# Three more groups of expert weights loaded inside attention layer 3, and the later groups spread over the experts' pairs

## The chip, the cores and the metric

The kernel runs on one core of one Trainium2 chip. The time is device microseconds (us) of one execution of the whole program. The time before is the median of six runs. One more execution was profiled; its trace has a record of each instruction on each engine.

## The reference

The model has four layers over 4 sequences of 256 tokens with 256 features (1024 tokens in all). Each layer is an attention (or a grouped transform) and a feed-forward part, each added to the running `x`. The change touches only what lies around the last two: attention layer 3 and the mixture of 64 experts after it, of which each token uses 8:

```python
x = x + _L3_xattn_ref(_layernorm(x), ctx, seg_ids, W_kvc, W_dq, W_uq, W_qr, W_uk, W_kr, W_uv, W_o)
x = x + _L3_ffn_ref(_layernorm(x), gate_w, gate_proj_w, up_proj_w, down_proj_w)
# in _L3_ffn_ref, with h = 256, I = 96, E = 64, K = 8:
router_logits = x @ gate_w
routing_weights, selected = jax.lax.top_k(router_logits, K)
routing_weights = softmax(routing_weights)
hidden_sorted = repeat(x, K)[order]            # rows of all choices, sorted by expert
gate = ragged_dot(hidden_sorted, gate_proj_w, group_sizes)
up   = ragged_dot(hidden_sorted, up_proj_w, group_sizes)
down = ragged_dot(silu(gate) * up, down_proj_w, group_sizes)
out  = sum(down[unsort].reshape(-1, K, h) * routing_weights[..., None], axis=1)
```

## The kernel before

**Two ways of ordering.** Everything up to the end of attention layer 3 is written as many small threads (`Flow`, L115). A planner in Python runs them at build time with estimated durations: it picks the next step by due time and by when its inputs are ready, and so fixes the order of the instructions on each engine. Shared buffers are handed out by roles; a thread that needs one waits in the plan until one is free. The experts (`experts`, L1973) are written out by hand, in a fixed order on each engine.

**Staging slots.** The role `stg` (L456) has nine buffers of 128 partitions by 2056 floats (`NSTAGE` = 9; 2056 is 8 rows of 257). Weights of the layers are loaded into them, and later the slots serve as queries of layer 3 (`q0`, `q1`) and as `hx`, the normalized rows that GpSimd scatters. The part `hx` may take slots 0 to 6 (`HX` = 7). After layer 3 the pool of slots is closed, and the experts' pool `moe` (L1750) lies over the same memory.

**From layer 3 to the experts.** Each of eight tiles of 128 tokens ends attention 3 in `tile3` (L1583): router, places of the choices (`slots`), then `scatter` (L1668), which issues eight indirect DMAs on GpSimd (L1674), one per choice, that put the token's row into the HBM array `hs`, sorted by expert. There are 64 of them. `fill_rows` (L427) loads the rows of one pair of experts from `hs`; it waits for the scatters of the choices that can lie there. SP, the engine that issues most loads, has the first three of these at the end of its list for the layers. Then follows a short stretch (L1781 to L1798): VectorE computes `late` and `over`, PE sums `over` (L1786), ScalarE writes `left_i`, all engines branch on it (the branch is for choices that found no place), and VectorE and ScalarE turn the logits `lgs` into routing weights.

**The experts.** The 64 experts' weights come in 16 groups of 4 (`GROUP`); a group is two DMAs, gate and up (768 KB) and down (384 KB), into a tile of 128 partitions by 2560 floats. Groups 0 and 1 (`FIRST` = 2) are loaded inside layer 3 into dead tensors (`cx`, `ctxT` and the weights of the layer 2 feed-forward; `first_experts`, L1316). The others go into a ring of `WEIGHTS` = 6 tiles `wt`. The loop goes over 32 pairs of experts; pair p uses group p // 2. On PE a turn of the loop is: gate and up of pair p (L1991), transposes of pair p + 1 (L1852), down of pair p - 1 (L1933), the other part of up of pair p (L1924), the rest of down of pair p - 1 (L1939). ScalarE computes silu (L1995) and copies `hbT` (L1856) and the results `yb` (L2006, L2010); VectorE multiplies `act` (L1928, L2002). GpSimd writes the results of a pair with three indirect DMAs (L1944) into the HBM array `yd`.

What follows a pair is in `beside` (L1955): it issues on SP the rows of pair p + 6 (`AHEAD`), perhaps a group of weights, perhaps a load of finished results from `yd` (`load_results`, L1862), and on VectorE some sums. The group's index is

```python
k = FIRST + 3 + p if p < WEIGHTS - 3 else p // 2 + WEIGHTS if p % 2 and p > 3 else 0
```

so that groups 5, 6 and 7 go after pairs 0, 1 and 2, and groups 8 to 15 after pairs 5, 7, 9 and so on to 19. Groups 2, 3 and 4 are issued ahead of the loop by `experts`. SP takes its list in order: a row load that must wait for its buffer (the rows of pair p + 6 take the buffer of pair p, which the result DMAs of pair p read) holds back the groups behind it.

Of the kernel before, what the change touches and what calls it, by code (L numbers as in the profile page):

```python
# [28 lines left out]
P = 128  # L29
B, S, D = 4, 256, 256  # L30
NTOK = B * S
NT = NTOK // P
# [14 lines left out]
E3, I3, K3 = 64, 96, 8  # L47
# [12 lines left out]
NROWS = E3 * CAP  # L60
NPAIR = NTOK * K3
NSTAGE = 9
HX = 7
HW = D + 1


# [48 lines left out]
class Flow:  # L115
# [11 lines left out]
    def role(self, name, n, make=None):  # L127
        self.roles[name], self.makers[name] = [0.0] * n, make

    def part(self, name, role, n):  # L130
        self.parts[name] = role, n

    def slots(self, name):
        role, n = self.parts.get(name, (name, None))
        return self.roles[role][:n]

    def go(self, gen, due=0.0):
        th = Thread(gen, due)
        self.threads.append(th)
        self.resume(th, None)  # L140
        return th
# [15 lines left out]
    def start(self, op):  # L157
        t = self.free.get(op.engine, 0.0)
        for b in op.reads:
            if b.ready is None:  # L160
                return None
            t = max(t, b.ready)
        for b in op.writes:
            t = max(t, b.used, b.ready or 0.0)
        need = {}
        for spec in op.new:
            need[spec[0]] = need.get(spec[0], 0) + 1
        for name, n in need.items():
            times = sorted(x for x in self.slots(name) if x is not None)
            if len(times) < n:  # L170
                return None
            t = max(t, times[n - 1])
        return t

    def take(self, spec):
        name, args = spec[0], spec[1:]
        k = min((x, k) for k, x in enumerate(self.slots(name)) if x is not None)[1]
        name = self.parts.get(name, (name,))[0]
        self.roles[name][k] = None
        make = self.makers[name]  # L180
        return Buf(make(k, *args) if make else None, name, k)
# [50 lines left out]
def model(ctx: ExitStack, tc: tile.TileContext, a: dict, out: bass.AP):  # L232
    nc = tc.nc
# [14 lines left out]
    def held(pool, shape, name, dtype=F32):  # L248
        return pool.tile(shape, dtype, tag=name, name=name)
# [40 lines left out]
    q2 = [held(early, [P, 2 * I2], f"q2{k}", BF16) for k in range(3)]  # L290
    means = held(early, [P, 8], "means")
    wmask = held(early, [P, NT, S], "wmask", BF16)
    kvc = held(const, [P, NT, KVC3], "kvc")
    kpos = held(early, [P, S], "kpos")
    mid = held(early, [P, NT], "mid")
# [97 lines left out]
    def expert_sources(k):  # L393
        es = slice(k * GROUP, (k + 1) * GROUP)
        return a["w3_gu"][:, es, :, :], a["w3_dn"][:, es, :]
# [5 lines left out]
        )  # L401
    ]

    readers = []
    puts = [[] for _ in range(K3)]

# [28 lines left out]
    def layers(nk):  # L435
# [11 lines left out]
            )  # L447

        def stage_tile(k, name):
            return stage.tile([P, K3 * HW], F32, tag=f"stg{k}", name=name)  # L450

        flow.role("bank", 8, maker(banks, "bank"))
# [2 lines left out]
        flow.role("sc", 32, maker(acts, "sc"))  # L455
        flow.role("stg", NSTAGE, stage_tile)  # L456
        flow.part("hx", "stg", HX)
        flow.role("lane", LANES[0])
        flow.role("lane3", LANES[1])

# [33 lines left out]
        def loader():  # L494
# [10 lines left out]
                    queue.dma_start(dst, source)  # L505

            def stage_in(name, kb, pairs):
                b = yield Op(SP, 0.06, new=[("stg", name)], kb=kb)
                for dst, source in pairs(b.ap):
                    nc.sync.dma_start(dst, source)  # L510
                fill(name, b)
# [60 lines left out]
            )  # L572
            yield from put(WROT, nc.sync, 384, (wrot3, a["w3_qrot"]))
            yield from put(GATE3, nc.sync, 64, (gate3, parts_of("w3_gate", 2)))
            b = yield Op(None, 0.0, new=[("stg", "keys3")])
            fill("keys3", b)
            yield from stage_in(
                "wq3", 384,
# [9 lines left out]
                    for k, n in enumerate(("w3_ukT", "w3_uvT"))  # L588
                ],
            )  # L590
            b = yield Op(None, 0.0, new=[("stg", "bo3")])
            fill("bo3", b)
            for k in range(2):
                yield from stage_in(
# [721 lines left out]
        def first_experts():  # L1316
            yield Join([keys_thread])
            for parts, k in first_weights:
                yield Op(SP, 0.12, (), (CX, *CT, *Q2), kb=1152)
                for dst, source in zip(parts, expert_sources(k)):  # L1320
                    nc.sync.dma_start(dst, source)

        waiting = [2] * B

        before = [len(js) for js in puts]
        PUT = [Buf() for _ in range(K3)]

        def first_rows():
            for p in range(in_early - 1):
                yield Op(SP, 0.06, PUT[2 * p : 2 * p + 2], kb=386)  # L1330
                fill_rows(p, before)
# [356 lines left out]
        def attention3(b):  # L1688
            lane = yield Op(None, 0.0, new=[("lane3",)])
            q = yield Op(None, 0.0, new=[("stg", "q0"), ("stg", "q1")])  # L1690
            yield from queries3(b, q)
            left = [2]
            for k in range(2):
                go(tile3(2 * b + k, q, lane, left), due(b, "h3") + 15.0 * k)

        with tc.manual_schedule(engines=ORDERED | {mybir.EngineType.SP}):
            go(loader())
            if nk == 1:
                few_thread = go(few_rows(), due(0, "x0"))
            for c in range(NCH):  # L1700
                go(chunk(c), due(2 * c, "x0"))
            w = DUE_WEIGHTS
            go(fp8_weights(), w["fp8"])
            go(scaled_context(), w["f1"] - 20.0)
            go(ffn1_weights(), w["f1"])
            go(products2(), w["p2"])
            go(ffn2_weights(), w["f2"])
            go(windows(), w["win"])
            go(centred_gate(), w["win"])
            keys_thread = go(keys_values(), w["kv"])  # L1710
            go(products3(), w["p3"])
            go(first_rows())
            flow.run()

# [37 lines left out]
    def moe_tile(shape, tag, bufs):  # L1752
        return moe.tile(shape, F32, tag=tag, name=tag, bufs=bufs)

    diag = moe_tile([P, NT // 2, len(ON_PE), P], "diag", 1)
    wts = [moe_tile([P, GROUP * (4 * I3 + D)], "wt", WEIGHTS)]
    weights = [parts for parts, _ in first_weights]

    def load_weights(k):
        wt = wts.pop() if wts else moe_tile([P, GROUP * (4 * I3 + D)], "wt", WEIGHTS)  # L1760
        parts = expert_parts(wt[:, : GROUP * 4 * I3], wt[:I3, GROUP * 4 * I3 :])
        for dst, source in zip(parts, expert_sources(k)):
            nc.sync.dma_start(dst, source)
        weights.append(parts)


    def load_rows(p):
# [66 lines left out]
    silu = small.tile([P, 1], F32, tag="silu", name="silu", bufs=1)  # L1834
    eqs = moe_tile([P, K3, E3], "eqs", 1)
    backs, gats = [], {}
    n_pairs = E3 // 2

    def choice_weights(t):
# [22 lines left out]
    def load_results(js, p):  # L1862

        half = NT // 2
        for h in range(2):
            if js[0] in (0, 2, 3) and (h == 0 or js[0] == 0):
                g = moe_tile([P, GROUP * (4 * I3 + D)], "wt", WEIGHTS)[:, : NT * D]
            elif js[0] == 4:
                g = gats[0][h].rearrange("p t j d -> p (t j d)")
            elif js[0] == 6:  # L1870
                g = (cx.rearrange("p t d -> p (t d)"), ctxT.rearrange("p c r -> p (c r)"))[h]
            else:
                continue
            g = g.rearrange("p (t j d) -> p t j d", j=len(js), d=D)
            n = 2 if js[0] == 6 else g.shape[1]
            for j in js:
                gats.setdefault(j, []).append(g)
            for t0 in range(0, g.shape[1], n):
                at = (h * half + t0) * P * K3
                source = yd[at : at + n * P * K3, :].rearrange("(t p j) d -> p t j d", p=P, j=K3)  # L1880
                ld = nc.sync.dma_start(  # L1881
                    g[:, t0 : t0 + n].rearrange("p t j d -> p t (j d)"),
                    source[:, :, js[0] : js[-1] + 1, :].rearrange("p t j d -> p t (j d)"),
                )
                needs(ld, "back", backs[: RPP * (p + 1)], "results of these choices alone")
# [69 lines left out]
    def beside(p):  # L1955
        if p < 2 * NT and p % 2 == 0:
            choice_weights(p // 2)
        n, m = len(on_pe), n_pairs - 2 * NT
        for t, j in on_pe[max(p - 2 * NT, 0) * n // m : max(p - 2 * NT + 1, 0) * n // m]:
            nc.vector.tensor_scalar(  # L1960
                diag[:, t // 2, j - ON_PE[0], :], ident, choice_w[:, t, j : j + 1], None, ALU.mult
            )
        if p + AHEAD < n_pairs:
            load_rows(p + AHEAD)
        k = FIRST + 3 + p if p < WEIGHTS - 3 else p // 2 + WEIGHTS if p % 2 and p > 3 else 0
        if k and k < E3 // GROUP:
            load_weights(k)
        if p in loaded:
            load_results(loaded[p], p)
        for t, j in added_at.get(p, ()):  # L1970
            add_result(t, j)

    def experts():  # L1973
        load_weights(FIRST)
        for p in range(in_early - 1, AHEAD):
            load_rows(p)
        load_weights(FIRST + 1)
        load_weights(FIRST + 2)

        nc.scalar.activation(silu, mhalf, AF.Silu)  # L1980
        nc.vector.tensor_mul(lgs, lgs, wide(kept))
# [148 lines left out]
```

## Time and profile before

| | us |
|---|---|
| median of 6 runs | 687.32 (685.62 to 689.4) |
| profiled execution, whole | 686.86 |
| its span from first to last instruction | 685.1 |
| PE matmul busy | 595.5 (87%) |
| VectorE, ScalarE, GpSimd busy | 427.1, 376.8, 411.5 |
| attention layer 3 ends, last scores (L1526) | 460.9 |
| last scatter ends on GpSimd (L1674) | 493.6 |
| first pair's gate and up (L1991) | 490.5 |
| last pair's gate and up (L1991) | 646.3 |

The share of the span that an engine is busy is a mean over stages with different limits; the windows view gives it by stretch. A row of the waits view says which engine's instruction on which line waited, and for what. A wait for several things is put down to the one that came last. Matmul ends are modelled. The granted clock of PE is between 0.5 and 1.

### The profile page before, as it was taken

What the parts mean: (1) busy time and instruction counts of PE and PEld (TensorE: products, weight loads), DVE (VectorE), ACT (ScalarE), POOL (GpSimd) and SP (SyncE); (2) the same over time, 40 slices, a digit from 0 to 9 for tenths busy, and PEclk for the clock granted to TensorE, in tenths of its full rate; (3) what the DMA queues carried; (4) which work ended last, traced back from release to release, by engine and by line L of the source; (5) the groups of instructions that cost most, each with busy time, mean ns of one, the idle gap of its engine ahead of it and who ended that gap; (6) DMA issues with size and microseconds to landing.
All of it is one profiled execution on the core that took longest, in us unless ns stands there. A gap on an engine that the chain in (4) does not pass through costs nothing. (4 is left out here: it accounts for less than half of the span.)

```text
span 685.1 us, 11045 instructions
## 1 busy us (share of the span) xinstructions
PE 595.5 (87%) x3703; PEld 451.8 (66%) x3716; DVE 427.1 (62%) x1063; ACT 376.8 (55%) x931; POOL 411.5 (60%) x531
## 2 busy tenths in 40 slices
PE   5997699989999999999999899496497998888936
PEld 4763376766887778778687678274375776766724
DVE  5789857875968795799785556353343453323625
ACT  1143258769788763667876875384344453434500
POOL 6997985044464536558268587727645666555860
PEclk9999999999999999999999999799599999999966
DMA  8999999501100230000031110202689788877376
GB/s 282 369 386 215 204 211 244 153 25 47 62 2 1 62 108 2 0 1 1 4 114 39 62 63 32 93 16 81 195 273 326 249 241 280 265 213 244 92 237 238
DMA packets 65250, 98.14 MB, mean 143 GB/s; under 512 B 7174, under 2 KB 51927, under 8 KB 65184
## 3 DMA queue, kind: packets, MB, share of 16 engines
q1 hardware_dynamic: 55264, 78.40, 40.0%
q0 software_dynamic: 7680, 16.84, 7.0%
q10 hardware_dynamic: 2240, 2.10, 0.9%
q8 instruction: 32, 0.52, 0.3%
q14 instruction: 34, 0.28, 0.1%
HBM read 58.42 MB, written 43.07 MB: 148 GB/s over the span
## 5 line engine op out<-in xcount | busy, mean ns | idle before, releaser
L1944 POOL DMA_INDIRECT yd<-yb,hb x84 | 92.2, 1098 | 52.1 <-issue 22.2
L1674 POOL DMA_INDIRECT hs<-hx,slots x64 | 66.0, 1032 | 26.0 <-issue 13.7
L881 POOL TENSOR_TENSOR st<-st,mhalf 128x1 f32<-128x1 f32 x56 | 33.0, 593 | 57.4 <-DVE st L877 43.5
L1928 DVE TENSOR_TENSOR act<-ps_u,g 64x192 f32<-64x192 f32 x64 | 22.7, 355 | 50.8 <-PE ps_u L1924 22.6
L1991 PE MATMUL ps_gu<-hbT,wt 128*128 128x192 f32 x224 | 44.4, 342 | 8.2 <-ACT hbT L1856 8.2
L1505 POOL TENSOR_TENSOR q<-rt 64x512 f32<-64x512 f32 x32 | 42.5, 1327 | 11.0 <-DVE rt L1501 7.7
L1991 PEld LDWEIGHTS ps_gu<-hbT,wt 128*128 128x128 f32 x224 | 35.9, 191 | 19.4 <-ACT hbT L1856 11.0
L1538 ACT ACTIVATE e<-ps_s,nm 128x128 f32<-128x128 f32 x128 | 45.6, 392 | 5.6 <-DVE nm L1532 4.8
L2002 DVE TENSOR_TENSOR act<-ps_gu,g 32x384 f32<-32x384 f32 x32 | 18.0, 562 | 41.0 <-ACT g L1995 31.5
L1995 ACT ACTIVATE g<-ps_gu 96x384 f32<-96x384 f32 x32 | 15.6, 487 | 42.6 <-PE ps_gu L1991 13.4
L1933 PE MATMUL ps_y<-wt,act 96*128 96x256 f32 x112 | 31.4, 406 | 8.4 <-DVE act L1928 6.6
L1526 PEld LDWEIGHTS ps_s<-keys,q 128*128 128x128 f32 x256 | 34.7, 197 | 1.4
L1526 PE MATMUL ps_s<-keys,q 128*128 128x128 f32 x256 | 34.6, 279 | 0.0
L1450 POOL TENSOR_TENSOR hh<-g,v 128x512 f32<-128x512 f32 x16 | 20.2, 1276 | 23.8 <-ACT g L1448 20.0
L1576 PE MATMUL ps_u<-e,kvc 128*64 128x512 f32 x64 | 22.8, 632 | 12.4 <-issue 10.1
L1856 ACT COPY hbT<-tp_hb 128x768 f32<-128x768 f32 x31 | 24.7, 798 | 14.7 <-PE tp_hb L1852 9.7
L1259 ACT ACTIVATE qT<-tp_q,rnd 128x512 bf16<-128x512 f32 (+2 forms) x48 | 25.7, 568 | 12.4 <-PE tp_q L1255 12.4
L1532 DVE TENSOR_REDUCE nm<-ps_s 128x4 f32<-128x512 f32 x32 | 21.5, 683 | 14.9 <-remote 11.2
L1491 PE MATMUL ps_q<-qc,wq 96*128 96x256 f32 x128 | 30.4, 380 | 0.0
L884 DVE TENSOR_SCALAR h<-x,st 128x256 f32<-128x256 f32 x56 | 27.0, 494 | 5.1 <-POOL st L881 4.8
L1163 ACT ACTIVATE e<-ps_s,nb 128x256 f32<-128x256 f32 x64 | 30.1, 494 | 0.0
L1562 ACT COPY e<-tp_e 128x512 f32<-128x512 f32 x32 | 18.5, 605 | 20.2 <-issue 10.4
(348 smaller groups left out, 1720.2 us busy)
## 6 DMA issues: line engine op xcount, KB each, us to landing
hs<-order SPq DMA_DIRECT2D x1, 12336.0 KB
hb<-hs SPq DMA_DIRECT2D x28, 385.5 KB
wt<-in_w_gu SPq DMA_DIRECT2D x14, 768.0 KB
yd<-order SPq DMA_DIRECT2D x1, 8192.0 KB
wt<-yd SPq DMA_DIRECT2D x6, 1024.0 KB
wt<-in_w_dn SPq DMA_DIRECT2D x14, 384.0 KB
wo<-in_w_o SPq DMA_DIRECT2D x2, 1024.0 KB
w<-in_w SPq DMA_DIRECT2D x2, 704.0 KB
```

Of the source, the lines that this page charges most:

```text
L881: nc.gpsimd.tensor_tensor(s[:, 8:9], s[:, 7:8], mhalf, ALU.pow)
L884: nc.vector.tensor_scalar(h[:, k, :], x_t(t), ss[k][:, 6:7], ss[k][:, 8:9], ALU.subtract, ALU.mult)
L1163: nc.scalar.activation(e[:, mt, :], s[:, mt, :], AF.Exp, bias=nb[:, mt : mt + 1], accum_out=tot[:, 2 * j + mt : 2 * j + mt + 1],)
L1259: nc.scalar.activation(qT[:, 4 * i : 4 * i + full, :], tp.ap[:, :full, :], AF.Identity, bias=rnd[:, 1:2])
L1491: nc.tensor.matmul(ps.ap[:, k, :], w[:, hp * P : (hp + 1) * P], qc.ap, start=True, stop=True)
L1505: nc.gpsimd.tensor_add(qv(q[i])[r, hps, :], t0[r], t1[r])
L1526: nc.tensor.matmul(s.ap[:, k, :], qv(q[hd % 2])[:, hd // 2, rows], keys3[:, hd % 2, b * S : b * S + nk * P], start=False, stop=k == n - 1,)
L1538: nc.scalar.activation(wide[:, k, :], s.ap[:, k, :], AF.Exp, bias=nm[:, k : k + 1], accum_out=tot[:, k : k + 1],)
L1674: put = nc.gpsimd.indirect_dma_start(out=hs[:, :], out_offset=bass.IndirectOffsetOnAxis(ap=slots[:, t, j : j + 1], axis=0), in_=rows[:, j, ...
L1933: nc.tensor.matmul(y[:, i], act[:, i, whole[i]], dn[:, i], start=True, stop=True)
L1944: put = nc.gpsimd.indirect_dma_start(out=yd[:, :], out_offset=bass.IndirectOffsetOnAxis(ap=hbs[p][:, j, D : D + 1].bitcast(I32), axis=0), ...
L1991: nc.tensor.matmul(ps[:, i], gu[:, i, dc, :P], hbT[:, dc, mine[i]], start=dc == 0, stop=dc == 1)
```

## The change

Four of the nine staging slots (7, 2, 6, 8, in this order) become one tensor, `deep`, that outlives the layers, so that three tiles of 2560 floats fit into it side by side. `more_experts` loads groups 2, 3 and 4 there inside layer 3: the first when slot 7 is given back, the second for slot 6, the third for slot 8, none before the queries of the last sequence are asked for (`ASKED`). So that the slots are free in time, `hx` may take only slots 0, 4 and 5, the kept tensors `keys3` and `bo3` slots 1, 3 and 5, and `wq3` slot 2. The ring of six tiles becomes a fixed list, `homes`: three in `deep` and three from the pool `moe`; group k uses home (k - 2) % 6. No group is issued ahead of the loop any more. Groups 5 to 15 are issued in `beside` after pairs 0, 3, 5, 8, 11, 14, 16, 19, 22, 24 and 27 (`round(2.7 * k)`). The tiles into which results are loaded come from the same list.

```diff
-HX = 7
+HX = (0, 4, 5)
+KEPT = (1, 3, 5)
+DEEP = (7, 2, 6, 8)
...
+    deep = held(early, [P, len(DEEP) * K3 * HW], "deep")
...
+    n_wt = GROUP * (4 * I3 + D)
+    homes = [deep[:, o : o + n_wt] for o in range(0, len(DEEP) * K3 * HW - n_wt + 1, n_wt)]
+
+    def home_parts(wt):
+        return expert_parts(wt[:, : GROUP * 4 * I3], wt[:I3, GROUP * 4 * I3 :])
+
+    def fetch(k, parts):
+        for dst, source in zip(parts, expert_sources(k)):
+            nc.sync.dma_start(dst, source)
...
         def stage_tile(k, name):
+            if k in DEEP:
+                o = DEEP.index(k) * K3 * HW
+                return deep[:, o : o + K3 * HW]
             return stage.tile([P, K3 * HW], F32, tag=f"stg{k}", name=name)
...
         flow.part("hx", "stg", HX)
+        flow.part("kept", "stg", KEPT)
+        flow.part("wq3", "stg", (2,))
+        for k in DEEP:
+            flow.part(f"deep{k}", "stg", (k,))
...
+        def more_experts():
+            for k, home in enumerate(homes):
+                taken = [f"deep{n}" for n in (DEEP[:1], DEEP[2:3], DEEP[3:])[k]]
+                yield Op(SP, 0.12, (ASKED,), new=[(n, "wt") for n in taken], kb=1152)
+                fetch(FIRST + k, home_parts(home))
...
             yield from queries3(b, q)
+            if b == B - 1:
+                ASKED.ready = flow.now
...
             go(products3(), w["p3"])
+            go(more_experts())
             go(first_rows())
...
-    wts = [moe_tile([P, GROUP * (4 * I3 + D)], "wt", WEIGHTS)]
+    homes += [moe_tile([P, n_wt], f"wt{k}", 1) for k in range(len(homes), WEIGHTS)]
     weights = [parts for parts, _ in first_weights]
-
-    def load_weights(k):
-        wt = wts.pop() if wts else moe_tile([P, GROUP * (4 * I3 + D)], "wt", WEIGHTS)
-        parts = expert_parts(wt[:, : GROUP * 4 * I3], wt[:I3, GROUP * 4 * I3 :])
-        for dst, source in zip(parts, expert_sources(k)):
-            nc.sync.dma_start(dst, source)
-        weights.append(parts)
+    weights += [home_parts(homes[k % WEIGHTS]) for k in range(E3 // GROUP - FIRST)]
...
+    free_homes = [homes[k % WEIGHTS] for k in range(E3 // GROUP - FIRST, E3 // GROUP - FIRST + 4)]
...
-                g = moe_tile([P, GROUP * (4 * I3 + D)], "wt", WEIGHTS)[:, : NT * D]
+                g = free_homes.pop(0)[:, : NT * D]
...
-        k = FIRST + 3 + p if p < WEIGHTS - 3 else p // 2 + WEIGHTS if p % 2 and p > 3 else 0
-        if k and k < E3 // GROUP:
-            load_weights(k)
+        if p in fetched:
+            fetch(fetched[p], weights[fetched[p]])
...
+    early_groups = FIRST + len(DEEP) - 1
+    fetched = {round(2.7 * k): early_groups + k for k in range(E3 // GROUP - early_groups)}
+
     def experts():
-        load_weights(FIRST)
         for p in range(in_early - 1, AHEAD):
             load_rows(p)
-        load_weights(FIRST + 1)
-        load_weights(FIRST + 2)
```

More of the change, by code (lines that the diff above doesn't have):

```diff
@@ L128, in role, with part @@
         self.roles[name], self.makers[name] = [0.0] * n, make
-    def part(self, name, role, n):
-        self.parts[name] = role, n
+    def part(self, name, role, ks):
+        self.parts[name] = role, ks
     def slots(self, name):
-        role, n = self.parts.get(name, (name, None))
-        return self.roles[role][:n]
+        role, ks = self.parts.get(name, (name, None))
+        times = self.roles[role]
+        return [(times[k], k) for k in (range(len(times)) if ks is None else ks) if times[k] is not None]
     def go(self, gen, due=0.0):
@@ L168, in start @@
         for name, n in need.items():
-            times = sorted(x for x in self.slots(name) if x is not None)
+            times = sorted(x for x, _ in self.slots(name))
             if len(times) < n:
@@ L176, in take @@
         name, args = spec[0], spec[1:]
-        k = min((x, k) for k, x in enumerate(self.slots(name)) if x is not None)[1]
+        k = min(self.slots(name))[1]
         name = self.parts.get(name, (name,))[0]
@@ L507, in stage_in @@
             def stage_in(name, kb, pairs):
-                b = yield Op(SP, 0.06, new=[("stg", name)], kb=kb)
+                b = yield Op(SP, 0.06, new=[("wq3" if name == "wq3" else "stg", name)], kb=kb)
                 for dst, source in pairs(b.ap):
@@ L574, in loader @@
             yield from put(GATE3, nc.sync, 64, (gate3, parts_of("w3_gate", 2)))
-            b = yield Op(None, 0.0, new=[("stg", "keys3")])
+            b = yield Op(None, 0.0, new=[("kept", "keys3")])
             fill("keys3", b)
@@ L590, in loader @@
             )
-            b = yield Op(None, 0.0, new=[("stg", "bo3")])
+            b = yield Op(None, 0.0, new=[("kept", "bo3")])
             fill("bo3", b)
@@ L1319, in first_experts @@
                 yield Op(SP, 0.12, (), (CX, *CT, *Q2), kb=1152)
-                for dst, source in zip(parts, expert_sources(k)):
-                    nc.sync.dma_start(dst, source)
+                fetch(k, parts)
+        def more_experts():
[3 more added lines that the diff above has]
+                fetch(FIRST + k, home_parts(home))
         waiting = [2] * B
+        ASKED = Buf()
         before = [len(js) for js in puts]
@@ L1755, in model @@
     diag = moe_tile([P, NT // 2, len(ON_PE), P], "diag", 1)
-    wts = [moe_tile([P, GROUP * (4 * I3 + D)], "wt", WEIGHTS)]
+    homes += [moe_tile([P, n_wt], f"wt{k}", 1) for k in range(len(homes), WEIGHTS)]
     weights = [parts for parts, _ in first_weights]
-    def load_weights(k):
-        wt = wts.pop() if wts else moe_tile([P, GROUP * (4 * I3 + D)], "wt", WEIGHTS)
-        parts = expert_parts(wt[:, : GROUP * 4 * I3], wt[:I3, GROUP * 4 * I3 :])
-        for dst, source in zip(parts, expert_sources(k)):
-            nc.sync.dma_start(dst, source)
-        weights.append(parts)
+    weights += [home_parts(homes[k % WEIGHTS]) for k in range(E3 // GROUP - FIRST)]
     def load_rows(p):
```

## The prediction

> **What bounds the kernel now.** I read the windows first (columns: stretch, its length, busy time with instruction count of PE, weight load, VectorE, ScalarE, GpSimd, then granted clock, DMA share, GB/s).
>
> ```profile
> 480.00:500.00 20.00, 10.65 (x48) 8.44 (x48) 6.82 (x15) 6.56 (x11) 11.31 (x21) 0.60 0.65 195
> 500.00:520.00 20.00, 17.66 (x123) 13.52 (x124) 9.04 (x18) 8.92 (x17) 11.38 (x12) 1.00 0.95 300
> 520.00:540.00 20.00, 16.14 (x113) 12.31 (x114) 8.48 (x17) 7.61 (x15) 10.90 (x12) 1.00 0.94 299
> 600.00:620.00 20.00, 16.39 (x113) 13.01 (x113) 5.49 (x16) 7.25 (x15) 10.75 (x12) 0.97 0.66 199
> ```
>
> To about 470 the layers run with PE 94 to 99% busy per 100 us from 100 to 400. The experts (488 to 660) are bound by PE too, but PE waits there, and at their start the DMA engines are full (0.95, 0.94). What PE waits for, from the waits view of 486 to 646 (us in total, times, longest):
>
> ```profile
> PE ps_gu L1991 <- ACT hbT L1856: 9.1, 7, 2.1
> PE tp_hb L1852 <- DMA q<-hs: 6.4, 1, 6.4
> PE tp_hb L1852 <- DMA hb<-hs: 2.7, 3, 1.7
> ...
> PE tp_hb L1852 <- DMA wmask<-hs: 0.9, 1, 0.9
> ```
>
> Then the timeline from layer 3 into the experts (start, duration, engine, line):
>
> ```profile
> 480.84 0.22 DVE L1781 TENSOR_TENSOR late<-tops,bound 128x64 f32<-128x64 f32 x1 [3.26 <-POOL tick L1673]
> 481.10 0.22 DVE L1784 TENSOR_REDUCE over<-late 128x8 f32<-128x64 f32 x1
> 483.37 0.69 DVE L1791 TENSOR_TENSOR q<-q,tops 128x512 f32<-128x512 f32 x1 [2.05 <-ACT left_i L1788]
> 488.21 0.69 DVE L1981 TENSOR_TENSOR q<-q,kept 128x512 f32<-128x512 f32 x1
> 490.51 0.56 DVE L1859 COPY hbT<-tp_hb 128x384 f32<-128x384 f32 x1 [1.61 <-issue]
> 490.53 2.93 PE L1991 MATMUL ps_gu<-hbT,cx 128*128 128x192 f32 x8 [0.57 <-issue]
> 492.60 0.98 POOL L1674 DMA_INDIRECT hs<-hx,slots  x1 [0.22 <-issue]
> 500.30 0.37 SPq L429 DMA_DIRECT2D wmask<-hs  x1
> ```
>
> The reader is to see: VectorE goes through `late` to L1981 (8.1 us) while GpSimd still issues scatters (the last ends at 493.58). Nothing in that chain waits for scatters to land. SP's load of pair 3 (`wmask`) does, and is issued only at 500.30.
>
> I call S(p) the start of pair p's first L1991. From S(9) = 538.35, S(10) = 542.60, S(11) = 546.86 an undisturbed pair takes 4.25 us. The sum is made against the profiled execution, 686.86 us (span 685.1 and 1.76 around it); the median of the runs, 687.32, lies 0.46 above.
>
> **What does not move.** In the built programs the instructions of PE, VectorE, ScalarE and GpSimd stand in the same order, and the planner gives the same staging slots to the same tensors. Cost to 480: nothing. What differs is SP's list and what some instructions wait for.
>
> **Three groups inside layer 3.** They sit in SP's list behind groups 0 and 1 and ahead of the first rows (issued 484.46). Their slots are last read by L1491 (412) and by the last scores, L1526 (460.9). A group takes about 6.5 us (issued at 593.70, hardware queue busy to about 600), DMA is 17% busy in 450 to 480, so all have landed by about 475. Cost nothing, hidden by SP's idle time before 484; were that cover gone, each group would put the first rows back by its 6.5.
>
> **Relief at the start.** Before, six groups leave SP from 492 to 518, mixed with the row loads; rows of pair 7, issued at 507.86, let PE start only at 524.46. After, no group is issued between layer 3 and `wmask`, rows of pairs 4 to 6 go next, and groups 5 and 6 follow. From S(0) = 490.53 to S(10) took 52.07. Without these waits it is 10.82 for the first two pairs (clock at 0.50 to 495) plus 8 x 4.25 = 44.8. So at most -7.2; the five waits that name rows or precede row-bound transposes (0.88, 0.61, 1.73, 1.09, 1.04) make -5.35. I take -6.3.
>
> **An added wait.** The experts' pool keeps three weight tiles instead of six, so its tiles sit elsewhere. In the built program the first VectorE instruction after layer 3, `late` (L1805 after), now waits for all eight counters of the scatters, six at their full count of 128, the last scatter's among them; before it waited for none. Queued behind it on VectorE are L1791 to L1798, L1981 and then L1859, the second half of `hbT` of pair 0. Waiting for those: the overflow matmul, which stands ahead of the first transposes on PE, ScalarE's exponentials, and the first L1991. So the experts cannot start before the last scatter has landed plus that chain.
>
> When does it land? GpSimd is done at 493.58. Upper bound: 500.2, where SP's 5.8 us wait for it ended before, with group 2's 1152 KB and 771 KB of rows on the same engines. Lower bound: rows of pairs 1 and 2 were issued 3.1 and 1.8 us after GpSimd ended the last scatter they need, so 495.4. Group 2 is gone, so I take 496.3, 2.7 after. The chain: 8.1 us at most (480.84 to 488.90), 6.1 if the 2.05 ahead of L1791, which no counter explains, passes during the wait. S(0) is then 502.4 to 504.4; I take 503.4, +12.9 on 490.53. Ends: 495.4 + 6.1 is +11.0, 500.2 + 8.1 is +17.8.
>
> **Later groups.** They are issued at p = 0, 3, 5, 8, 11, 14, 16, 19, 22, 24, 27, each behind the row load of p + 6, which waits until the results of pair p are written. Group 15 was issued after pair 19, used at 30. Those row loads left 13.5, 13.3, 11.4, 12.3, 14.4 and 10.6 after S(p+1) (p = 20 to 25), median 12.8; 0.5 for the issue and 5 for the gate and up part makes 18.3. Group 12 (p = 19, pair 24) has 4 x 4.25 = 17.0: 1.3 late. Group 13 (p = 22, pair 26) has 12.75: 5.5 late, but S(23) to S(26) took 16.60 anyway, leaving 1.65. Group 14 is covered by 13's delay; group 15 follows row load 31 (p = 25) and is in time. So 2.9 to 6.8; take +4. Bounds: 0 if results land in 10, and 10 with the clock's drop on two waits (after the 2.1 us wait at 576.37 the clock stood at 0.50 in 578 to 581, and S(17) to S(18) took 5.88, 1.6 too long).
>
> [...]
>
> **What stays.** S(10) to S(31) took 103.66 against 21 x 4.25 = 89.25: 14.4 of waits, mostly `hbT` from ScalarE, whose cause the rows do not show. From S(31) to the end, 38.8: result writes of GpSimd back to back from 634 to 664.7, then the loads of results. I keep both, within 4 either way.
>
> Sum: 686.86 + 12.9 - 6.3 + 4 = 697.5; on the median 697.9.
>
> **Rivals.** (1) Relief decides and it is faster. Place: scatters landing at 495.4, chain 6.1: +11.0; relief in full, -7.2; no late group; and half of the 14.4 gone, since three groups fewer share the engines: -7.2. That gives 683.5. It decides once waits of the stage fall by more than the 11.0 that the start loses. For it: DMA share 0.8 to 0.95 there. Against: S(9) to S(11) ran at 4.25 each with the DMA share at 0.79 (540 to 560). (2) The late groups become the bound: landing at 498 and chain 8.1 (+15.6), relief -5.35, late groups +10: 707. It decides if results land 14 us after S(p+1), as once. Against: the spread of the six. (3) The added wait is already met when VectorE gets there, so that only relief and late groups count: 686.86 - 6.3 + 4 = 684.6. Against: 480.84 lies 12.7 us ahead of the last scatter's issue.
>
> **How the numbers follow.** Forecast 0.76, rival 1 0.08, rival 2 0.13, rival 3 0.03. The forecast's own range is 690.7 to 704.1 (686.86 with 11.0 - 7.2 + 0 and with 15.6 - 5.35 + 7). To hold 8 in 10 it takes a part of rivals 1 and 2 at each end: 688.5 to 706. A difference of 0.3%, 2.1 us, is about what a measurement of this kernel can tell from none. Faster by more: rival 1 and 0.01 of rival 3, 0.09; within: 0.02 of rival 3 and 0.04 at the edge of the forecast, 0.06; slower 0.85.
>
> **What would show it.** Right: `late` starts at 495 to 498, S(0) at 502 to 505, no wait of L1852 for `hb` before pair 10, S(10) at 547 to 551, and PE waiting for weights (`ps_gu` behind `deep` or `wt` loads) around pairs 24 to 28. Wrong: `late` near 481, or S(0) within 5 us of 490.5; or a layer before 480 whose lines move; or S(10) to S(31) in under 96, which would be rival 1's saving.

## The result and the profile after

The changed kernel takes 705.64 us (median of 20 runs, 700.44 to 710.17) against 687.09 before; the ratio is 1.0289, 95% interval 1.0264 to 1.0314. On the 687.32 from which the forecast started that is 707.2, 1.2 above the upper end of the forecast range and 9.3 above the forecast of 697.9. The direction was right and the size was not. Times are us throughout. The profiled execution took 703.76, span 702.0.

The same four stretches as before, and one more behind them (stretch, length, PE, weight load, VectorE, ScalarE, GpSimd, granted clock, DMA share, GB/s):

```profile
480.00:500.00 20.00, 0.00 (x0) 0.01 (x1) 1.13 (x6) 2.47 (x3) 13.07 (x26) 0.50 0.48 150
500.00:520.00 20.00, 16.37 (x91) 12.30 (x92) 9.61 (x20) 9.53 (x16) 3.30 (x4) 0.76 0.90 269
520.00:540.00 20.00, 18.25 (x126) 14.42 (x127) 9.21 (x20) 8.64 (x17) 12.05 (x13) 1.00 0.15 50
600.00:620.00 20.00, 15.72 (x102) 12.59 (x99) 5.23 (x15) 6.75 (x13) 11.67 (x12) 0.91 0.70 231
...
636.00:643.00 7.00, 6.20 (x22) 5.28 (x24) 0.56 (x1) 1.56 (x3) 2.21 (x3) 0.51 0.75 243
```

PE does nothing at all from 480 to 500, where it was busy for 10.65 before. From 520 to 540 the DMA engines are nearly idle (0.15, before 0.94) and PE is busier (18.25, before 16.14). The last line is new: PE at half clock (0.51) late in the experts. The waits of 480 to 665 (us in total, times, longest) name both ends:

```profile
PE ps_over L1810 <- DVE over L1808: 20.5, 1, 20.5
...
DVE late L1805 <- DMA hs<-hx,slots: 18.8, 1, 18.8
...
PE ps_gu L2015 <- ACT hbT L1881: 10.1, 6, 4.3
...
PE ps_gu L2015 <- DMA wt<-in_w_gu: 4.0, 1, 4.0
...
PE ps_gu L2015 <- DMA deep<-in_w_gu: 3.6, 1, 3.6
```

The timeline from the last scatter to the first pair (L2015 is the gate and up line of after, L2005 the old L1981):

```profile
495.23 0.97 POOL L1701 DMA_INDIRECT hs<-hx,slots  x1 [0.23 <-issue]
498.87 0.36 SPq L443 DMA_DIRECT2D wmask<-hs  x1
499.39 0.23 DVE L1805 TENSOR_TENSOR late<-tops,bound 128x64 f32<-128x64 f32 x1 [18.77 <-DMA hs<-hx,slots]
...
504.21 1.01 PE L2015 MATMUL ps_gu<-hbT,cx 128*128 128x192 f32 x2 [0.57 <-ACT hbT L1883]
...
504.61 0.69 DVE L2005 TENSOR_TENSOR q<-q,kept 128x512 f32<-128x512 f32 x1
```

The last scatter ends on GpSimd at 496.20; 3.2 later `late` runs, and 4.8 after that PE starts pair 0. With S(p) read from the rows of L1991 and L2015, the difference of the two profiled spans (16.9) splits like this; the last column repeats it for a second trace of each kernel, both taken on one chip in the same group of runs:

| stretch | before | after | difference | forecast | second pair of traces |
|---|---|---|---|---|---|
| to S(0) | 490.53 | 504.21 | +13.7 | +12.9 | +10.8 |
| S(0) to S(10) | 52.07 | 48.02 | -4.1 | -6.3 | -3.7 |
| S(10) to S(31) | 103.66 | 114.05 | +10.4 | +4 | +10.0 |
| S(31) to the end | 38.84 | 35.72 | -3.1 | 0 | -1.2 |

### The profile page after: what moved, and what is told of

Its sections match the earlier page's. It is cut to its first block, busy times and chain, and to the rows that moved or that the text cites. A ratio compares the mean times of both kernels' runs of the same rounds, so it can differ in the third digit from the quotient of the medians.

```text
span 702.0 us, 11054 instructions
## 1 busy us (share of the span) xinstructions
PE 600.1 (85%) x3703; PEld 455.3 (65%) x3716; DVE 425.4 (61%) x1063; ACT 376.2 (54%) x931; POOL 409.0 (58%) x531
## 5 line engine op out<-in xcount | busy, mean ns | idle before, releaser
L1969 POOL DMA_INDIRECT yd<-yb,hb x84 | 90.0, 1072 | 58.3 <-issue 23.2
L1701 POOL DMA_INDIRECT hs<-hx,slots x64 | 65.3, 1021 | 26.6 <-issue 13.7
L2019 ACT ACTIVATE g<-ps_gu 96x384 f32<-96x384 f32 x32 | 15.6, 486 | 51.3 <-PE ps_gu L2015 17.2
L2015 PE MATMUL ps_gu<-hbT,deep 128*128 128x192 f32 x128 | 26.6, 353 | 10.0 <-ACT hbT L1881 5.9
L2015 PEld LDWEIGHTS ps_gu<-hbT,deep 128*128 128x128 f32 x128 | 21.5, 198 | 16.6 <-issue 8.3
L1280 ACT ACTIVATE qT<-tp_q,rnd 128x512 bf16<-128x512 f32 (+2 forms) x48 | 25.7, 567 | 10.8 <-PE tp_q L1276 10.7
L1518 PE MATMUL ps_q<-qc,deep 96*128 96x256 f32 x128 | 30.4, 380 | 0.0
L1532 POOL TENSOR_TENSOR deep<-rt 64x512 f32<-64x512 f32 x20 | 27.2, 1361 | 5.5 <-DVE rt L1528 2.7
L1589 ACT COPY e<-tp_e 128x512 f32<-128x512 f32 x32 | 18.4, 609 | 21.5 <-remote 11.1
L1565 ACT ACTIVATION_READ_ACCUMULATOR e<-ps_s,nm 128x1 f32 x128 | 29.8, 233 | 0.0
L1622 PE MATMUL ps_y<-bo,u 128*128 128x256 f32 x128 | 29.4, 383 | 0.0
L1119 PE MATMUL ps_g<-hT,w_gate 128*128 128x512 bf16 x69 | 21.1, 447 | 8.0 <-ACT hT L1099 4.3
```

What stands on the lines that cost most here:

```text
L1280: nc.scalar.activation(qT[:, 4 * i : 4 * i + full, :], tp.ap[:, :full, :], AF.Identity, bias=rnd[:, 1:2])
L1518: nc.tensor.matmul(ps.ap[:, k, :], w[:, hp * P : (hp + 1) * P], qc.ap, start=True, stop=True)
L1532: nc.gpsimd.tensor_add(qv(q[i])[r, hps, :], t0[r], t1[r])
L1565: nc.scalar.activation(wide[:, k, :], s.ap[:, k, :], AF.Exp, bias=nm[:, k : k + 1], accum_out=tot[:, k : k + 1],)
L1622: nc.tensor.matmul(y.ap, u[:, hp, :], bo3[:, hp, :], start=hp == 0, stop=hp == H3 // 2 - 1)
L1701: put = nc.gpsimd.indirect_dma_start(out=hs[:, :], out_offset=bass.IndirectOffsetOnAxis(ap=slots[:, t, j : j + 1], axis=0), in_=rows[:, j, ...
```

## The experiments

**The overlap alone.** In the changed kernel the last slot of `hx` covers bytes 155584 to 163808 of a partition and `late` starts at 163648: they share 160 bytes. A tile that nothing uses moves `late` behind it.

```diff
+    held(moe, [P, 64], "pad")
     late = held(moe, [P, NT, K3], "late")
```

> The changed kernel with one unused tile of 256 bytes per partition ahead of `late` in the experts' pool, so that `late` starts at byte 163904 instead of 163648 and no longer shares its first 160 bytes with the last slot of `hx`. Theory A (that overlap alone makes VectorE wait for the last scatter): `late` runs near 481, S(0) falls from 504.2 to 490 to 492, S(10) to S(31) stays near 114, and the kernel takes 690 to 694, about 13 less than the changed kernel's 705.6. Rival B (something else holds the start, the rows of the first pairs or ScalarE's part, and only the name of the wait changes): S(0) stays at 500 or later and the time at 702 to 707.

Measured: 697.4, ratio 1.0147 (1.0091 to 1.0204), about 9.8 less than the changed kernel's 1.0289. The timelines of VectorE and PE in this kernel:

```profile
483.07 0.23 DVE L1806 TENSOR_TENSOR late<-tops,bound 128x64 f32<-128x64 f32 x1 [2.93 <-issue]
```

```profile
493.17 2.93 PE L2016 MATMUL ps_gu<-hbT,cx 128*128 128x192 f32 x8 [0.57 <-ACT hbT L1884]
```

The 18.8 of waiting are gone and S(0) is 11.0 earlier. Theory A holds for the cause. The time fell by less than the 13 that it gave (with four runs the interval of the gain, some 4 either way, still holds 13); in the trace S(0) to S(10) grew from 48.02 to 51.03, with a wait of 3.28 for `hbT` ahead of pair 9.

**The late groups alone.**

```diff
-    fetched = {round(2.7 * k): early_groups + k for k in range(E3 // GROUP - early_groups)}
+    fetched = {0: 5, 3: 6, 4: 7} | {2 * k - 11: k for k in range(8, E3 // GROUP)}
```

> The changed kernel with groups 5, 6, 7 issued after pairs 0, 3, 4 and groups 8 to 15 after pairs 5, 7, 9 and so on to 19, as the kernel before does; all else stays. Theory A (the late groups cost what the stretch of S(10) to S(31) grew by, 10.4, and the last pairs give back some 3 because results are read later): no wait of L2015 for weights, S(10) to S(31) near 104 instead of 114, S(0) still near 504, time 695 to 699. Rival B (the stretch is long for another reason, the engines' transfers or PE's slow answers in the middle): S(10) to S(31) stays above 110 and the time above 702.

Measured: 696.18, ratio 1.0123 (1.005 to 1.0195), about 11.4 less than the changed kernel. No wait of L2015 for weights is left, S(10) to S(31) is 105.76 instead of 114.05, S(0) is 503.45. Theory A.

**Both together** (the two diffs above).

> Both edits: the unused tile ahead of `late`, and the groups issued as early as in the kernel before. Only the relief at the start is left of the change. Theory A (the two costs are separate and add up): S(0) near 491, S(10) near 538 to 540, S(31) near 643, time 680 to 685, that is 2 to 7 below the kernel before. Rival B (rows and weights meet again as soon as the experts start earlier, so that the relief was only lent by the late start): S(0) to S(10) back at 51 to 53 and the time within 2 of the kernel before.

Measured: 685.96, ratio 0.9988 (0.9952 to 1.0023). The two gains by ratio, 1.42 and 1.66 points, add up to 3.08; together they gave 3.01. Each of the two gains is known to some 0.6 or 0.8 points, so the closeness is partly luck; but the interval of the ratio leaves at most 0.5 points for anything else in the change. So the two costs are separate, as theory A has it, but on the time, by the ratio, rival B holds (within 2 of the kernel before). S(0) to S(10) is 49.61, between the two, and S(10) to S(31) 102.83.

**Why a group is late: the row load ahead of it.** In `beside` the group is issued ahead of the rows.

```diff
-        if p + AHEAD < n_pairs:
-            load_rows(p + AHEAD)
         if p in fetched:
             fetch(fetched[p], weights[fetched[p]])
+        if p + AHEAD < n_pairs:
+            load_rows(p + AHEAD)
```

> The changed kernel with the same pairs for the groups, but in each pair the group is issued ahead of the rows of pair p + 6 instead of behind them. Theory A (a group is late because the row load in front of it waits some 12.8 us for results): groups 13 and 14 leave 10 to 13 earlier, the two waits of L2015 for weights at pairs 26 and 28 vanish or fall under 1 us, S(10) to S(31) 103 to 107, time 695 to 700. Rival B (group 14 is late because the loads of finished results stand ahead of it on the DMA engines): the wait at pair 28 stays at 2 to 4 us and the time falls by less than 6, to 700 or more.

Measured: 701.68, ratio 1.0232 (1.0154 to 1.0311). Pair 26 no longer waits for weights, but pair 28 waits twice as long. Its timelines of SP and PE:

```profile
632.76 0.49 SPq L1906 DMA_DIRECT2D deep<-yd  x1
633.36 0.44 SPq L1906 DMA_DIRECT2D wt<-yd  x1
633.84 0.51 SPq L416 DMA_DIRECT2D deep<-in_w_gu  x1
```

```profile
648.50 2.90 PE L2015 MATMUL ps_gu<-hbT,deep 128*128 128x192 f32 x8 [7.52 <-DMA deep<-in_w_gu]
```

Group 14 leaves right behind the two result loads of 1024 KB each and is 14.7 on its way (633.84 to 648.50). Theory A holds for group 13 and rival B for group 14, whose wait even grew past the 2 to 4 that rival B gave it.

**Why a group is late: the results ahead of it.** The changed kernel with the first load of results moved behind group 14:

```diff
-        loaded[last] = js
+        loaded[last + (js == LOADS[0])] = js
...
-            load_results(loaded[p], p)
+            load_results(loaded[p], p - (loaded[p] == LOADS[0]))
```

> The changed kernel, but the first load of finished results (two loads of 1024 KB) is issued after pair 24, behind group 14, instead of after pair 23, ahead of it; it still waits for the same results. Theory A (group 14 is late because these 2 MB stand ahead of it): its landing moves from about 651.5 to about 649, the wait at pair 28 falls from 3.6 to under 1.5, pair 26 keeps its wait of 3 to 4, and the time falls by 2 to 5, to 701 to 704. Rival B (the issue time of the group alone decides): pair 28 waits 3 or more as before and the time stays at 704 to 708.

Measured: ratio 1.0267 (1.0225 to 1.0308), on a chip where the kernel before takes 655.93, so that only ratios and stretches compare. PE's timeline at pairs 26 and 30:

```profile
605.42 2.01 PE L2015 MATMUL ps_gu<-hbT,wt 128*128 128x192 f32 x8 [3.20 <-DMA wt<-in_w_gu]
...
627.84 2.90 PE L2015 MATMUL ps_gu<-hbT,deep 128*128 128x192 f32 x8 [3.44 <-DMA deep<-in_w_gu]
```

Pair 28 no longer waits, but pair 30 now does, for group 15. The two result loads left SP at 609.49 and 610.19 and group 15 at 619.78, 14.4 after S(26), behind its row load; PE had the weights at 627.84, 8.1 after their issue. So the 2 MB now stand ahead of group 15; how much of its wait is theirs and how much the row load's, this run does not separate. Theory A names the place rightly; the gain that it promised is passed on to the next group, and the ratio is the changed kernel's within the intervals.

**The same two costs put into the kernel before**, on that same chip. First the wait: `late` is laid at the start of `diag`, which lies on a slot of `hx`.

```diff
-    late = held(moe, [P, NT, K3], "late")
+    late = diag[:, 0, 0, : NT * K3].rearrange("p (t k) -> p t k", t=NT)
```

> The kernel before with one line changed: `late` is put at the start of the tile `diag`, which lies on a slot of `hx`, so that VectorE waits there for the last scatter as in the changed kernel. Theory A (the wait costs the same here): `late` at 496 to 500, S(0) at 501 to 505 instead of 490.5; of these 11 to 14 a part comes back, since rows and groups 2 to 7 have that time to land (S(0) to S(10) 46 to 49 instead of 52), time 693 to 698. Rival B (all comes back, as the start is bound by the transfers): S(10) at 543 to 545 and the time within 3 of the kernel before.

Measured: ratio 1.0104 (1.0073 to 1.0134), 6.8 on this chip: theory A. Its timeline:

```profile
486.02 0.23 DVE L1781 TENSOR_TENSOR diag<-tops,bound 128x64 f32<-128x64 f32 x1 [20.46 <-DMA hs<-hx,slots]
```

S(0) is 490.83, against 475.93 in a kernel of the same group of runs without the wait (the next but one); S(0) to S(10) is 45.47 against its 50.18. So 4.7 of 14.9 come back by the late start alone, with no group loaded early. (1.9 of the 14.9 is not the wait: the last scatter ended at 480.69 here and at 478.75 there.) The changed kernel with its result loads moved has the late start and the early groups, and takes 45.61 there: the early groups add nothing.

Then the late groups:

```diff
-        k = FIRST + 3 + p if p < WEIGHTS - 3 else p // 2 + WEIGHTS if p % 2 and p > 3 else 0
+        k = {round(2.7 * n): FIRST + 3 + n for n in range(11)}.get(p, 0)
```

> The kernel before with one line changed: groups 5 to 15 are issued after pairs 0, 3, 5, 8, 11, 14, 16, 19, 22, 24 and 27, as in the changed kernel. Theory A (the late issue costs the same in either kernel): L1991 waits for weights at pairs 26 and 28, S(24) to S(31) grows from 35 to 42 to 45, the start stays, or loses a few us of waits since fewer groups leave before 520, and the time is 692 to 698. Rival B (only together with the later start or the new places): time within 3 of the kernel before.

Measured: ratio 1.0072 (1.0036 to 1.0108), 4.7, the lower edge of what was expected (692.3 on the time of the forecast). The waits view:

```profile
PE ps_gu L1991 <- DMA wt<-in_w_gu: 9.6, 4, 4.5
```

The waits are there (3.57 at pair 26, 4.51 at pair 28), and S(24) to S(31) is 42.41 against 30.65 in the kernel below. The profiled execution, 666.28, is the slowest of the nine runs (657.17 to 666.28), so what the groups cost differs from run to run; the trace shows a dear one. Theory A for the mechanism, with a smaller price than in the changed kernel. The two costs add up to 1.8 points here; the changed kernel with its result loads moved lost 2.7 on this chip.

**The three early groups undone.** As the kernel with both edits, but groups 2, 3 and 4 are loaded ahead of the loop.

```diff
-                fetch(FIRST + k, home_parts(home))
...
     def experts():
+        fetch(FIRST, weights[FIRST])
         for p in range(in_early - 1, AHEAD):
             load_rows(p)
+        fetch(FIRST + 1, weights[FIRST + 1])
+        fetch(FIRST + 2, weights[FIRST + 2])
```

> The kernel of the last run (unused tile ahead of `late`, groups 5 to 15 issued early), but groups 2, 3 and 4 are loaded where the kernel before loads them, ahead of the experts' loop, into the same places; the order on PE, VectorE, ScalarE and GpSimd is the same. It shows what the three groups inside layer 3 are worth alone. Theory A (they cost 2 to 3 in layer 3, where `late` came at 483.1 and 483.3 instead of 480.8, and bring 2.5 to 4 at the start): `late` at 480.5 to 481.5, S(0) 490 to 491.5, S(0) to S(10) 52 to 54, time within 2 of the kernel before. Rival B (the slip of 2.5 is of the new staging or of the run, not of the transfers): `late` stays at 483, S(0) at 493, and with the rows late again the time is 688 to 692.

Measured: ratio 0.997 (0.9947 to 0.9993). PE waits 4.7 for `hb` in the first pairs, as before the change. Theory A's time is right (2.0 below, by the ratio); its places cannot be read on this chip, where all of layer 3 is some 15 earlier. With the early groups the ratio was 0.9988, without them, on another chip, 0.997, and the intervals overlap: what they bring by themselves is not to be told from nothing.

**Once more on one chip.**

> The kernel before, once more with a trace, on the same chip as the next three, since the last two groups of runs were on chips on which the same kernel took 688.9 and 655.9. Expected if the difference lies in PE's unexplained pauses (9.6 us near 431 and 14.4 in S(10) to S(31) in the first trace): on a chip where it takes about 656, no PE pause near 431 and S(10) to S(31) near 91; on one where it takes about 688, both as in the first trace. Time within 0.3% of the kernel before.

> The changed kernel once more, with a trace on the same chip as the kernel before. Theory A (the loss is the wait of `late` and the late groups): S(0) later by 11 to 14, S(0) to S(10) shorter by 4 to 5, S(24) to S(31) longer by 7 to 12, in all 2.5 to 3% slower than the kernel before on either kind of chip. Rival B (part of the loss is the pauses of PE, which fall otherwise in the changed kernel): on the faster chip less than 2%.

Measured: the kernel before 687.67, ratio 1.0022 (0.9985 to 1.0059); the changed one 706.03, ratio 1.0293 (1.0249 to 1.0338). The pauses of the kernel before are like those of its first trace, as expected for a chip of this time: one of 10.4 in layer 3 (9.6 before; it ends at 449.31 here and at 444.75 there, not near 431), and S(10) to S(31) takes 104.17. `late` in the first and in the second, from VectorE's timelines:

```profile
485.76 0.23 DVE L1781 TENSOR_TENSOR late<-tops,bound 128x64 f32<-128x64 f32 x1 [3.20 <-POOL tick L1673]
```

```profile
500.95 0.23 DVE L1805 TENSOR_TENSOR late<-tops,bound 128x64 f32<-128x64 f32 x1 [19.52 <-DMA hs<-hx,slots]
```

The kernel before has `late` at 485.76 here and had it at 480.84 in its first trace: layer 3 alone differs by 4.9 between two executions. VectorE stands idle from 482.56 in the one kernel and from 481.43 in the other, so the groups loaded in layer 3 do not delay it. (On the chip of 655.93 the last scatter ended at 478.60 with groups loaded early and at 477.64 to 480.69 in the three traces without.) Theory A on the time and on S(24) to S(31), 43.10 against 34.46; S(0) came 10.8 later, just less than its 11 to 14, and S(0) to S(10) fell by 3.7, just less than its 4 to 5. Rival B speaks of the faster chip, where the changed kernel itself was not run; the 2.7% that its variant lost there speaks against it.

**Both edits again, and group 5 behind more rows.** The first is the kernel with both edits; in the second group 5 goes after pair 2 instead of 0.

> The kernel with the unused tile and the early groups again, to see what the three groups inside layer 3 bring where both costs are gone. Theory A (relief): S(0) to S(10) 46 to 48 against 50 to 52 of the kernel before, the time 0.3 to 1% below the kernel before. Rival B (the relief is eaten by a later end of layer 3): `late` 2 to 3 later than in the kernel before, time within 0.3% of it.

> As the kernel just above, with group 5 issued after pair 2 instead of pair 0, so that the rows of pairs 4 to 8 stand ahead of all weights. Theory A (what is left of waits in the first ten pairs is rows behind groups 5 and 6): the wait ahead of S(4), 1.1 us, goes, and the time falls by 0.5 to 1.5 against it. Rival B (those rows are in time already): the same time within 0.5.

Measured: 0.9995 (0.9962 to 1.0028) and 1.0007 (0.9982 to 1.0033). Rival B on the time in the first: no relief is left that a measurement can tell (the interval allows at most 2.6). In the traces the stretch S(0) to S(10) is 49.03 and 51.12, shorter than the 54.14 of the kernel before on this chip but not the 46 to 48 of theory A. The second is 1.0 slower by the medians, inside the noise, so the place of group 5 shows no effect, and theory A's gain of 0.5 to 1.5 did not come. The waits ahead of S(4), 0.86 and 1.14, are for `hbT`, not for rows. `late` at 485.12 does not bear out rival B's reason.

## Why the prediction was right and wrong

**The added wait: right, by terms that were not all right.** `late` at 499.4 was forecast for 495 to 498, S(0) at 504.2 for 502 to 505. The landing, 3.2 after the last scatter's end, was taken as 2.7. The chain was taken as 7.1 and is 4.8: the first matmuls of pair 0 need ScalarE's half of `hbT` alone and start before L2005; only the other six wait for VectorE, until 505.82. What made up for it is luck: layer 3 ended 2.6 later (scatters until 496.20, not 493.58), which the second pair of traces shows to be the execution and not the change, for there it ended 1.9 earlier after the change (497.00 against 498.85). Counted from the last scatter's end the term is +11.1 in the first pair and +12.6 in the second, within the 11.0 to 17.8. (The 12.7 of rival 3 runs from `late` to the end of the last scatter on GpSimd; to its start it is 11.8. Nothing hangs on it.)

**The relief: too large, and of two causes.** Taken -6.3, bounds -5.35 to -7.2; measured -4.1 and -3.7. The waits for rows did go (the DMA share of 520 to 540 fell from 0.94 to 0.15), but other losses stood in their place: the first two pairs took 11.42, not 10.82, and the turns of pairs 3, 6 and 8 were 0.9, 1.3 and 0.45 too long, with a wait of 0.80 for ScalarE's `hbT` in one and an idle PE (0.86) that the trace puts down to nothing in another. And the relief is not the early groups' alone: the kernel before with the late start and its old groups shortened the stretch by 4.7, as much as both together on that chip. Nor is it the late start's alone: with the early groups and no late start four traces have 49.03 to 51.12, against the 52.07 and 54.14 of the kernel before. Either brings most of it, and the two do not add up. The start was costed and the relief was costed, and I did not see that the first pays for the second.

**The later groups: the step that failed.** Taken +4, with 2.9 to 6.8 worked out and 10 as the outer bound; measured +10.4 and +10.0. Against the forecast sum of +10.6, the spans give +16.9: of the 6.3 between, this term makes 6.4, the relief 2.2, the start 0.8, and the end takes 3.1 off. Timelines of SP and PE after:

```profile
630.44 0.52 SPq L416 DMA_DIRECT2D wt<-in_w_gu  x1
...
638.58 0.49 SPq L1906 DMA_DIRECT2D deep<-yd  x1
639.50 0.36 SPq L1906 DMA_DIRECT2D wt<-yd  x1
...
642.38 0.49 SPq L416 DMA_DIRECT2D deep<-in_w_gu  x1
```

```profile
636.80 2.90 PE L2015 MATMUL ps_gu<-hbT,wt 128*128 128x192 f32 x8 [3.96 <-DMA wt<-in_w_gu]
643.96 1.57 PE L2015 MATMUL ps_gu<-hbT,wt 128*128 128x192 f32 x8
651.90 1.73 PE L2015 MATMUL ps_gu<-hbT,deep 128*128 128x192 f32 x8 [3.62 <-DMA deep<-in_w_gu]
657.78 1.57 PE L2015 MATMUL ps_gu<-hbT,deep 128*128 128x192 f32 x8
```

Three parts of that step broke.

- Cover that was none. Group 13 was to come 18.3 after S(23) and came 17.7 after (619.08 to 636.80), 20.1 in the second trace. The sum was near by luck: it left 11.4 after, not 13.3, and took 6.4, not the 5 that the forecast gave for the gate and up part without a row (7.9 in the second trace). I let 16.60 of it be hidden, as S(23) to S(26) took so long before. But that stretch held a pause of 2.10 of unknown cause ahead of S(25) and half clock behind it (0.50 from 618.74 to 622.15); in this execution both fell elsewhere (a pause of 4.28 at pair 21, half clock from 608.74), pair 26 could have started at 632.8, and PE waited 4.0 instead of 1.65 (5.5 in the second trace). Group 12, which was to add 1.3, made no wait of weights at all.
- A neighbour in the queue. Group 14 was called covered by 13's delay, with 5 for its gate and up part. On the forecast's own numbers 1.0 was left even so: S(25) to S(28) took 15.66 before, and with 1.65 more that is 17.3 of the 18.3. It took 9.5 (642.38 to 651.90): 2 MB of results had been issued 3 to 4 ahead (638.58 and 639.50), and the DMA engines were full (share 1.02 from 642.4 to 651.9). The two experiments on the order show this from both sides.
- The clock, which stood in the outer bound alone. After the first wait it was 0.51 from 636 to 643, after the second 0.72 from 651 to 657, and S(26) to S(27) and S(28) to S(29) took 7.16 and 5.88, 2.9 and 1.6 too long. No run separates this part from the waits.

In sum the pairs from S(25) to S(29) lost 4.0 + 2.9 + 3.7 + 1.6 = 12.3, where before lost 2.9 there: 9.4 of the 10.4. In the second pair of traces the same pairs lost 13.3 and 2.6.

**What stays: right.** The end moved by 3.1 and 1.2, within the 4; layer 3 is not delayed. **Rival 2** named the size (707) and the price of the groups (10), but got there by a start of +15.6 that did not come; its condition, results landing 14 after S(p+1), was not needed: groups 8 to 14 left 11.4 to 14.8 after it, median 12.05. Rivals 1 and 3 are out.

**The clock.** The drop to 0.50 followed waits of 4.28, 3.96 and 3.62 here, and two waits of 2.1 in the trace of before; after the wait of 2.39 ahead of 558.94 the clock stayed at 1.00. So in these two traces the length of the wait does not decide. Where it lies tells them apart: between S(0) and S(31) the stretches at 0.50 that begin there last 3.41 (from 577.78 and 618.74 before, 608.74 and 653.11 after) or twice that (from 636.05 after). The stretches at 1.00 that end with a drop last a multiple of 3.41 too (81.92 and 37.55 before; 98.99, 23.90 and 10.23 after). Cut into steps of 3.41, what goes with the drop in them is PE's idle time within one step. The two steps around the first wait of 2.1 in before (columns as above), and the two around 558.94 after:

```profile
574.37:577.78 3.41, 1.41 (x9) 1.39 (x10) 1.27 (x3) 2.05 (x4) 1.15 (x2) 1.00 0.90 272
577.78:581.19 3.41, 3.41 (x13) 2.56 (x13) 0.56 (x1) 1.50 (x3) 2.22 (x3) 0.50 0.87 300
```

```profile
557.53:560.95 3.42, 2.01 (x14) 1.99 (x15) 0.87 (x3) 1.92 (x4) 0.99 (x2) 1.00 0.49 143
560.95:564.36 3.41, 3.41 (x25) 2.56 (x24) 1.98 (x5) 1.89 (x4) 2.80 (x3) 1.00 0.91 340
```

The wait of 2.1 lies almost whole in one step, which is idle for 2.00; the wait of 2.39 is cut in two by the border at 557.53, and 1.41 falls into the step shown. In these two traces, between S(0) and S(31), 5 whole steps at full clock had 2.0 or more of idle PE (2.00 and 2.10 before; 3.41, 3.22 and 2.20 after), and half clock followed each of them; one had 1.83 (591.43 to 594.84 before) and 77 had less than 1.75, and it followed none. That is a count over two traces; what sets the clock they do not show.

## What to carry to other kernels

When a pool or a slot moves, list what the first instruction of each engine in the next stage now waits for: 160 shared bytes of a tile that holds 256 cost about 10 us here, and an unused tile of 256 bytes took it away. Price a late transfer with what was issued ahead of it, other loads included: the gate and up part of group 14 took 9.5 with 2 MB of results issued 3 to 4 ahead of it and 14.7 right behind them, where group 13's took 6.4. A pause whose cause the trace does not show is no cover: the 2.10 within S(23) to S(26) before was not there in the execution after, which had 4.28 at pair 21.

## What the runs showed of the hardware

The same program takes 655.93 on one chip and 686.78 to 688.91 in the other groups of runs, and the traces show where. These waits are of 100 to 460, in the kernel before on a chip where it takes 686.78, and in its version with late groups on the chip of 655.93:

```profile
PE ps_u L1576 <- ACT e L1562: 10.4, 1, 10.4
```

```profile
PE ps_u L1576 <- ACT e L1562: 3.0, 2, 2.2
```

The wait of 2.2 is in both (in the first under another line of ScalarE), the pause of 10 in the first alone. Two traces of the chip of 655.93, the kernel before with late groups and with the wait, lack it (2.2 is the longest); six of the others have it: the two of the kernel before with 9.6 and 10.4, the two of the changed kernel and the two of the last experiments with 10.3 each. S(10) to S(31) takes 90.7 to 91.0 on that chip where no group is late, against 103 to 106 on the others and 89.25 undisturbed. So the 14.4 of waits that the forecast could not explain are pauses that these traces of one chip lack and those of the others have. What causes them stays open. No trace of the unchanged kernel was taken on the chip of 655.93.
